# Moving a decay table's construction into an earlier stage, and reordering a layer change

## The chip, the core and the metric

The kernel runs on one core of a Trainium2 chip. The core has five engines with a queue each, and each takes its instructions in order: TensorE (PE, matrix products and transposes; PEld is its weight load), VectorE (DVE), ScalarE (ACT), GpSimd (POOL), and SyncE (SP), which mostly issues DMA transfers. ACT and POOL can issue DMAs as well. An instruction that waits for a semaphore holds back everything behind it on its engine. The metric is the device time of one execution in microseconds.

## The reference, cut to what matters

The input is x with 4 sequences of 2048 rows of 512 numbers. Four sublayers follow, each added to x.

```python
x = x + attn_a(layernorm(x), ...)   # causal linear attention, 16 heads of 64
x = x + ffn(layernorm(x), rhs)      # rows quantized to int8 levels, product with quantized rhs
x = x + attn_b(layernorm(x), ...)   # 16 heads, state of 16 x 32 with decay
x = x + ffn(layernorm(x), rhs)
```

Layer b's attention is a recurrence over time:

```python
decay = sigmoid(base_decay_logits)            # one number for each of 16 heads x 16 rows
M = M * decay + outer(g_t * k_t * scale, v_t)
y = einsum('bhr,bhrd->bhd', q_t, M)
```

In chunks of 128 steps it needs powers of the decay: a chunk's queries and keys are multiplied by powers of it, or of its inverse.

## The kernel before, in words

The program runs two layers one after the other: `layer_a_mild` (attention a and the first ffn), then `layer_b_mild` (attention b and the second ffn). A tile scheduler places the instructions on the engines: it keeps each engine's work near the order in which it is written, but moves instructions by its own estimate of when they can start. Line numbers in this text (L126, L804) are those of the kernel before.

Layer a works on 16 blocks of 512 rows (`TA`), each as 4 row tiles of 128 (`NTA`). For each block it loops over 8 pairs of heads, `hp`. A pair has a short list of steps from `attend` (keys, scores, update, weigh, outputs); `spread` puts other work between them, the list `fill`: the next pair's features (`pk`, `pq`), the values (`pv`), the projection of the block before (`po`). In the middle of a block the next block's rows enter (`enter_row`: statistics, normalization) and are turned. The statistics end on POOL: `rs`, by an add (L126) and a power (L127). DVE then normalizes with it (L131). DVE also evicts the features: `kT` and `qT` (L804), which PE's scores `pss` (L888) read. POOL adds up the states `within` (L914). In block 0, the ffn's weights are loaded and quantized as well (`load_part`, `quantize_part`).

The ffn on a row tile is `ffn_levels` on DVE (normalize, largest magnitude, levels `f_q`), then a turn of `f_q` by a DMA on SP's queue (L676), the product `pf` (L681), `f_y` on DVE (L683) and the residual add on POOL (L684). For the last block these four come one after the other behind the last projections: the drain. There the weights' denominators come by way of DRAM (`rec`, then two broadcast loads), and the block is stored to `mmid` (L998) at the end.

Layer b works on 32 blocks of 256 rows (`TB`), 2 row tiles (`NTB`) and 2 groups of 8 heads (`G`) each. Its tiles lie on the memory of layer a's, so a load can wait for layer a's last use of that memory. Before its loop comes a prologue: loads of rows (`xb`), of query and key weights (`m_qT`, `m_kT`), gates, low-rank weights, small constants, values and output weights; then normalization and transposes of blocks 0 and 1, `fill_tables`, and block 0's features (`pr`, L1222), gates (`pg`), low-rank products (`pl`, L1255) and values (`pvb`).

`fill_tables` builds five tables for each group: `up` and `down` (powers 0 to 128, ascending and descending), `inv` (powers of the inverse to 64), `tq` and `tk` (put together from those). It doubles: each step multiplies the columns known so far by the last of them, a per-partition scalar:

```python
nc.vector.tensor_scalar(
    tab[:, g, n + 1 : 2 * n + 1], tab[:, g, 1 : n + 1],
    tab[:, g, n : n + 1], None, ALU.mult,
)
```

Of the kernel before, what the change touches and what calls it, by code (L numbers as in the profile page):

```python
# [33 lines left out]
G = 2  # L34
# [7 lines left out]
QB = 128  # L42
NQ = P // QB


@with_exitstack
def hybrid_block_kernel(ctx: ExitStack, tc: tile.TileContext, t: dict, out: bass.AP):
# [584 lines left out]

    class Block:
# [39 lines left out]
    def ffn_product(pool, bank, x, q, s1):  # L673

        qT = pool.tile([P, KC, P], BF16, name="f_qT", bufs=2)
        nc.sync.dma_start_transpose(qT, q)  # L676

        def product():
            pf = bank([P, D], F32, name="pf", tag="mm")
            for c in range(KC):  # L680
                nc.tensor.matmul(pf, qT[:, c, :], rq[:, c, :], start=(c == 0), stop=(c == KC - 1))  # L681
            y = pool.tile([P, D], F32, name="f_y", bufs=1)
            nc.vector.scalar_tensor_tensor(y, pf, s1, rscale, ALU.mult, ALU.mult)  # L683
            nc.gpsimd.tensor_tensor(x, x, y, ALU.add)  # L684

        return [product]
# [28 lines left out]
    def join_halves(dst, turned):  # L715

        nc.scalar.copy(  # L717
            dst.bitcast(U16).rearrange("p n (t two) -> p n t two", two=2),
            turned.rearrange("p (two n) t -> p n t two", two=2),
        )  # L720

    def layer_a_mild():
        with ExitStack() as es:
# [268 lines left out]
            def levels(B, i):  # L992
                row = B.x[:, i, :]
                B.mul[i] = ffn_product(pool, bank, row, *ffn_levels(pool, row))

            def store(B):
                m = dram.tile([TA, D], F32, name=f"mmid_{B.n}")
                nc.sync.dma_start(rows(m, 0, TA), B.x)  # L998
# [13 lines left out]
            for n in range(len(at)):  # L1012
# [6 lines left out]
                for hp in range(NP):  # L1019
# [18 lines left out]
                    if more and 0 <= hp - 2 < NTA:  # L1038
                        enter_row(after, hp - 2)
                    for place, f in zip((6, 7, 13, 15), weights):  # L1040
# [12 lines left out]
                if n:  # L1053
                    store(prev)
                prev = B
                B = after if more else None

# [3 lines left out]
            levels(prev, 0)  # L1061
            run(row[1][4:])
            levels(prev, 1)
            run(row[2][4:] + row[3][:4] + prev.mul[0])
            levels(prev, 2)
            run(row[3][4:] + prev.mul[1])
            levels(prev, 3)
            run(prev.mul[2] + prev.mul[3])
            store(prev)

    def layer_b_mild():
        with ExitStack() as es:

            late = es.enter_context(tc.tile_pool(name="mb_l", bufs=1, reuse_waits="tile"))
            soon = es.enter_context(tc.tile_pool(name="mb_s", bufs=1, reuse_waits="tile"))
            rowp = es.enter_context(tc.tile_pool(name="mb_r", bufs=2, reuse_waits="tile"))
            w = es.enter_context(tc.tile_pool(name="mb_w", bufs=1, reuse_waits="tile"))
# [5 lines left out]
            def load_x(n):  # L1083
                b, blk = at[n]
                x = rowp.tile([P, NTB, D], F32, name="xb", bufs=6)

                queue = nc.scalar if n < 2 else nc.sync
                queue.dma_start(x, rows(mids[b, blk * TB // TA], blk * TB % TA, TB))
# [8 lines left out]

            first_rows = [row_tiles()]
            xs = [load_x(n) for n in range(2)]
            wp = {"q": load_weight(soon, "m_qT", D), "k": load_weight(soon, "m_kT", D)}  # L1100
            wg = load_weight(soon, "b_gT", G * P)
            low = {}
# [3 lines left out]
            small = {}  # L1106
            for name in ("b_gb", "b_decay", "head4", "diag", "causal"):
                small[name] = w.tile(list(t[name].shape), F32, name=f"m_{name}")
                nc.sync.dma_start(small[name], t[name])
            nc.sync.dma_start(wv, t["b_vT"].rearrange("(c p) n -> p c n", p=P))  # L1110
            out_b, ln_g, ln_b = (load_row(w, name) for name in ("b_out_b", "b_ln_g", "b_ln_b"))
            nc.sync.dma_start(wo, t["b_oT"].rearrange("(c p) n -> p c n", p=P))
            H2 = QB // 2
            up = w.tile([P, G, P + 1], F32, name="up")
            down = w.tile([P, G, P + 1], F32, name="down")
            inv = w.tile([P, G, H2 + 1], F32, name="inv")
            lam = w.tile([P, G], F32, name="lam")
            ilam = w.tile([P, G], F32, name="ilam")
            tq = w.tile([P, G, QB], F32, name="tq")
            tk = w.tile([P, G, NQ, P], F32, name="tk")  # L1120

            def fill_tables():

                nc.scalar.activation(lam, small["b_decay"], AF.Sigmoid)
                nc.vector.reciprocal(ilam, lam)
                nc.vector.memset(up[:, :, 0:1], 1.0)
                nc.vector.memset(inv[:, :, 0:1], 1.0)
                nc.vector.memset(down[:, :, P : P + 1], 1.0)
                nc.vector.tensor_copy(up[:, :, 1:2], lam.unsqueeze(2))
                nc.vector.tensor_copy(inv[:, :, 1:2], ilam.unsqueeze(2))  # L1130
                nc.vector.tensor_copy(down[:, :, P - 1 : P], lam.unsqueeze(2))
                n = 1
                while n < P:
                    for g in range(G):
                        for tab, last in ((up, P), (inv, H2)):
                            if n < last:
                                nc.vector.tensor_scalar(
                                    tab[:, g, n + 1 : 2 * n + 1], tab[:, g, 1 : n + 1],
                                    tab[:, g, n : n + 1], None, ALU.mult,
                                )  # L1140
                        nc.vector.tensor_scalar(
                            down[:, g, P - 2 * n : P - n], down[:, g, P - n : P],
                            down[:, g, P - n : P - n + 1], None, ALU.mult,
                        )
                    n *= 2


                nc.gpsimd.memset(tk, 0.0)
                nc.vector.tensor_copy(tq[:, :, H2:QB], up[:, :, 0:H2])
                nc.vector.tensor_copy(tq[:, :, H2 - 1 : H2], ilam.unsqueeze(2))  # L1150
                n = 1
                while n < H2:
                    for g in range(G):
                        nc.vector.tensor_scalar(
                            tq[:, g, H2 - 2 * n : H2 - n], tq[:, g, H2 - n : H2],
                            tq[:, g, H2 - n : H2 - n + 1], None, ALU.mult,
                        )
                    n *= 2
                for j in range(NQ):
                    m = QB * j + H2  # L1160
                    nc.vector.tensor_copy(tk[:, :, j, 0:m], down[:, :, P - m : P])
                    nc.vector.tensor_copy(tk[:, :, j, m : m + H2], inv[:, :, 0:H2])

# [11 lines left out]
            def enter_row(B, i):  # L1175

                if i == 0:
                    blk = at[B.n][1]
                    B.cs = []
                    for name in ("cos", "sin2"):  # L1180
                        c1 = rowp.tile([P, TB], F32, name=f"m_{name}", bufs=3)
                        queue = nc.scalar if B.n < 2 else nc.sync
                        queue.dma_start(c1, t[name][:, blk * TB : (blk + 1) * TB])
                        B.cs.append(c1.unsqueeze(1).to_broadcast([P, 2, TB]))
# [6 lines left out]
            def turn_row(B, i):  # L1191
                dst = B.xnT[:, :, i * P : (i + 1) * P]
                if B.n > 1:
                    join_halves(dst, B.halves[i])
                else:
                    transpose_rows(bank, dst, B.xr[:, i, :])
                nc.gpsimd.tensor_tensor(B.x[:, i, :], B.x[:, i, :], ln_b, ALU.add)
# [70 lines left out]
            def prepare(B, g):  # L1268
# [4 lines left out]
                A.k1 = pool.tile([P, NTB, NQ, P], F32, name=f"k1{g}", bufs=1)  # L1273
                nc.vector.tensor_tensor(
                    A.k1,
                    k.rearrange("p (i s) -> p i s", s=P).unsqueeze(2).to_broadcast([P, NTB, NQ, P]),
                    tk[:, g, :, :].unsqueeze(1).to_broadcast([P, NTB, NQ, P]), ALU.mult,
                )
                qs = pool.tile([P, NTB * NQ, QB], F32, name="qs", bufs=1)
                nc.vector.tensor_tensor(  # L1280
                    qs, q.rearrange("p (j s) -> p j s", s=QB),
                    tq[:, g, :].unsqueeze(1).to_broadcast([P, NTB * NQ, QB]), ALU.mult,
                )
                A.q1 = pool.tile([P, NTB * NQ, 4, QB], F32, name=f"q1{g}", bufs=1)
# [12 lines left out]
            def chunk(B, i, g):  # L1297
# [10 lines left out]
                def scores():  # L1308

                    A = B.prep[g]  # L1310
                    ps = [bank([P, NQ, 4, QB], F32, name="ps", tag="s") for _ in range(2)]
                    for j in range(NQ):
                        for half in range(2):
                            r = slice(half * 64, (half + 1) * 64)
                            nc.tensor.matmul(  # L1315
                                ps[half][:, j, :, :], A.k1[r, i, j, :], A.q1[r, NQ * i + j, :, :],
                                start=True, stop=True,
                            )
                    C.a = pool.tile([P, 2, 4, P], F32, name="ab")
                    for half in range(2):  # L1320
                        nc.vector.tensor_tensor(
                            C.a[:, half, :, :].rearrange("p h (j s) -> p h j s", s=QB),
                            ps[half].rearrange("p j h s -> p h j s"),
# [245 lines left out]
```

## Time and profile before

| | us |
|---|---|
| median of 3 runs | 4071.2 (4069.48 to 4073.05) |
| the profiled execution's own time | 4069.52 |
| its span, first to last instruction | 4067.7 |
| PE busy in the span | 3971.8 |
| DVE / ACT / POOL busy | 2334.7 / 876.2 / 1486.8 |
| layer a's last block stored (`mmid`, issued) | 2446.8 |
| layer b's block 1 begins on PE | 2504.3 |

Times in the text are microseconds from the start of the span. A row of the timeline gives start, duration, engine, line, operation, the tile written and the tiles read; in brackets how long the engine was idle before it and what ended that. The chain of waits is followed back from the last instruction: at each step to what released it. The granted clock is that of TensorE, 1.00 at full speed; it was 0.991 on the mean of the run.

### The profile page before, as it was taken

The page shows a single profiled execution, that of the slowest core. Times are in us where ns is not written, and L with a number is a line of the kernel's source. Part 1 is how long each engine was busy: PE and PEld are TensorE (multiplying, and loading weights), DVE is VectorE, ACT ScalarE, POOL GpSimd, SP SyncE. Part 2 cuts the span into 40 slices and gives each one's busy share as a digit, 9 for nine tenths or more (in the row PEclk, how much of TensorE's full clock was granted, in tenths as well). Part 3 has the DMA queues.
Part 4 walks back from the last instruction along what each step waited for, and adds up shares of the span by engine and source line. Part 5 has one row for each costly group of instructions (what it writes and reads, how often), then busy time and mean ns, then how long its engine had stood idle before and what let it go on. Part 6 is the DMA issues. An engine that isn't in the chain of part 4 may idle for free.

```text
span 4067.7 us, 53656 instructions
## 1 busy us (share of the span) xinstructions
PE 3971.8 (98%) x20821; PEld 2147.3 (53%) x20821; DVE 2334.7 (57%) x4556; ACT 876.2 (22%) x1420; POOL 1486.8 (37%) x2527
## 2 busy tenths in 40 slices
PE   8999999999999999999999987999999999999997
PEld 4554554555555555555555544555555555555553
DVE  4455555555555555555555454666666666666665
ACT  2122222221221222222122111222222222222221
POOL 3223323323333323323332223444444454444443
PEclk9999999999999999999999998999999999999998
DMA  4112212212212222221221123112211121221211
GB/s 135 32 39 58 64 36 62 60 38 64 55 43 64 54 54 52 54 66 38 54 66 39 39 65 108 47 47 49 51 47 47 47 50 48 50 50 47 53 32 29
DMA packets 432041, 217.25 MB, mean 53 GB/s; under 512 B 363808, under 2 KB 376992, under 8 KB 431776
## 3 DMA queue, kind: packets, MB, share of 16 engines
q1 hardware_dynamic: 430656, 212.16, 21.3%
q8 instruction: 165, 2.70, 0.3%
q10 hardware_dynamic: 1120, 1.57, 0.1%
q14 instruction: 100, 0.82, 0.1%
HBM read 91.49 MB, written 34.08 MB: 31 GB/s over the span
## 4 chain that ended last, share of the span: by engine, by line
PE 82%; DVE 8%; POOL 7%; issue 1%; DMA 1%; ACT 0%; SPq 0%; POOLq 0%; ACTq 0%; DVEq 0%
PE pk L648 11%; PE pv L648 11%; PE pq L648 11%; PE po L648 10%; PE pr L1222 8%; PE py L648 5%; PE pss L888 3%; PE pn L974 3%; PE pvb L648 3%; PE pn L968 3%; PE pf L681 2%; PE pu L904 2%; PE ps L1315 2%; PE pl L1255 2%; PE pg L648 2%; POOL rs L127 2%
## 5 line engine op out<-in xcount | busy, mean ns | idle before, releaser
L648 PE MATMUL pq<-xnTa,a_Wq 128*128 128x512 f32 x1024 | 492.2, 608 | 0.0
L648 PE MATMUL pk<-xnTa,a_Wk 128*128 128x512 f32 x1024 | 491.0, 604 | 0.0
L648 PE MATMUL pv<-a_Wv,xnTa 128*128 128x512 f32 x1024 | 475.3, 602 | 2.9 <-ACT xnTa L141 2.9
L648 PE MATMUL po<-a_Wo_sb,oT 128*128 128x512 f32 x1024 | 467.1, 601 | 6.1 <-DVE oT L950 6.1
L126 POOL TENSOR_SCALAR rs<-mv 128x1 f32<-128x1 f32 x320 | 70.7, 221 | 764.2 <-DVE mv L125 763.9
L914 POOL TENSOR_TENSOR within<-state,u 64x64 f32<-64x64 f32 x256 | 154.5, 603 | 524.6 <-ACT u L909 515.0
L648 PEld LDWEIGHTS po<-a_Wo_sb,oT 128*128 128x128 f32 x1024 | 189.5, 191 | 234.3 <-issue 220.9
L648 PEld LDWEIGHTS pv<-a_Wv,xnTa 128*128 128x128 f32 x1024 | 188.4, 190 | 233.7 <-issue 223.7
L648 PEld LDWEIGHTS pq<-xnTa,a_Wq 128*128 128x128 f32 x1024 | 181.4, 189 | 193.1 <-issue 182.8
L648 PEld LDWEIGHTS pk<-xnTa,a_Wk 128*128 128x128 f32 x1024 | 184.6, 190 | 180.8 <-issue 158.8
L909 ACT COPY u<-pu 128x256 f32<-128x256 f32 x128 | 47.6, 372 | 1027.6 <-PE pu L904 1016.7
L1222 PE MATMUL pr<-xnTb,m_kT_sb 128*128 128x256 f32 x1024 | 259.5, 392 | 0.0
L1222 PE MATMUL pr<-xnTb,m_qT_sb 128*128 128x256 f32 x1024 | 252.8, 390 | 0.0
L648 PE MATMUL pvb<-b_vT_sb,xnTb 128*128 128x512 f32 x512 | 242.3, 606 | 0.0
L894 DVE TENSOR_TENSOR sm<-pss,causal 128x512 f32<-128x512 f32 x256 | 164.3, 683 | 119.9 <-PE pss L888 119.9
L648 PE MATMUL py<-b_oT_sb,yT 128*128 128x512 f32 x512 | 231.6, 594 | 0.0
L717 ACT COPY kr<-turned 128x1024 uint16<-128x1024 uint16 x120 | 139.3, 1161 | 425.4 <-DMA turned<-planes 425.4
L1222 PEld LDWEIGHTS pr<-xnTb,m_qT_sb 128*128 128x128 f32 x1024 | 187.5, 190 | 77.0 <-issue 44.5
L1222 PEld LDWEIGHTS pr<-xnTb,m_kT_sb 128*128 128x128 f32 x1024 | 184.4, 189 | 51.2 <-issue 20.0
L1361 POOL TENSOR_TENSOR state_b<-pairs,m_diag 128x256 f32<-128x256 f32 x128 | 98.3, 768 | 293.5 <-DVE pairs L1339 187.1
L127 POOL TENSOR_TENSOR rs<-rs,neg_half 128x1 f32<-128x1 f32 x320 | 193.7, 606 | 23.8
L838 DVE TENSOR_TENSOR xa<-po,xa 128x512 f32<-128x512 f32 x64 | 44.1, 689 | 260.1 <-PE po L648 260.1
(158 smaller groups left out, 6412.5 us busy)
## 6 DMA issues: line engine op xcount, KB each, us to landing
wide<-rec SPq DMA_DIRECT2D x124, 256.0 KB, 3.7
mmid<-xa SPq DMA_DIRECT2D x16, 1024.0 KB, 4.3
out<-xb SPq DMA_DIRECT2D x32, 512.0 KB, 2.8
xa<-in_x SPq DMA_DIRECT2D x15, 1024.0 KB, 6.3
xb<-mmid SPq DMA_DIRECT2D x30, 512.0 KB, 3.8
turned<-planes SPq DMA_TRANSPOSE x304, 3.1
m_cos<-in_cos SPq DMA_DIRECT2D x30, 128.0 KB, 2.3
m_sin<-in_sin SPq DMA_DIRECT2D x30, 128.0 KB, 2.3
```

Source lines behind the costliest of these rows:

```text
L127: nc.gpsimd.tensor_tensor(rs, rs, neg_half[:, :n], ALU.pow)
L648: nc.tensor.matmul(held[0], lhs(), rhs(), start=(n == 0), stop=(n == len(pairs) - 1))
L681: nc.tensor.matmul(pf, qT[:, c, :], rq[:, c, :], start=(c == 0), stop=(c == KC - 1))
L717: nc.scalar.copy(dst.bitcast(U16).rearrange("p n (t two) -> p n t two", two=2), turned.rearrange("p (two n) t -> p n t two", two=2),)
L888: nc.tensor.matmul(ps[h][:, i, :], k[r, chunks[i]], q[r, chunks[i]], start=True, stop=True)
L894: nc.vector.tensor_tensor(s, ps[h], causal.unsqueeze(1).to_broadcast([P, NTA, P]), ALU.mult)
L904: nc.tensor.matmul(pu[r, i, :], A.kr[:, i, r], v()[:, i, vh[h]], start=True, stop=True, skip_group_check=True,)
L914: nc.gpsimd.tensor_tensor(A.before[i + 1][r, r], A.before[i][r, r], u[r, i, :], ALU.add)
L968: nc.tensor.matmul(pn[:, i, :], A.before[i], q[:, chunks[i]], start=(i == 0), stop=False, skip_group_check=True,)
L974: nc.tensor.matmul(pn[r, i, :], v()[:, i, vh[h]], A.sm[h][:, i, :], start=False, stop=True, skip_group_check=True,)
L1222: nc.tensor.matmul(pr[:, half, :], wp[name][:, c, lo : lo + P], B.xnT[:, c, :], start=(c == 0), stop=(c == KC - 1),)
L1361: nc.gpsimd.tensor_tensor(st.rearrange("p (q c) -> p q c", c=2 * DB), pairs[:, g, :].unsqueeze(1).to_broadcast([P, HG // 2, 2 * DB]), smal ...
```

## The change

It has four parts.

1. `fill_tables` goes. A class `Powers` builds `up`, `down`, `inv` and `tq` in layer a's block 0, on POOL, in a piece of the tile `wide`; the steps are put between those of pairs 0 to 2 (`braid` mixes them into `fill`). SP stores the result to DRAM, and layer b loads it in one transfer. Layer b makes `tk` alone, by two copies on DVE.
2. In the drain, `f_q` is turned by PE and an ACT copy (`by_dma` false), not by a DMA; the steps are regrouped; the last store of `mmid` is issued by POOL.
3. Layer b's loads are reordered, and all stand on SP: rows, query weight and angles of block 0 first, tables and values later, the output weight last. `xb` and the angles get a pool of their own.
4. The prologue works block 0 first; block 1's rows enter between block 0's groups, and the residual adds (`residuals`) come after. The constants `QB`, `NQ` (128 and 1) go, which changes no shape.

The diff, cut to its core:

```diff
-    def ffn_product(pool, bank, x, q, s1):
+    def ffn_product(pool, bank, x, q, s1, by_dma=True):
         qT = pool.tile([P, KC, P], BF16, name="f_qT", bufs=2)
-        nc.sync.dma_start_transpose(qT, q)
+        if by_dma:
+            nc.sync.dma_start_transpose(qT, q)
         def product():
+            if not by_dma:
+                transpose_rows(bank, qT, q, BF16)
...
+    class Powers:
+        sizes = (P + 1, P + 1, H2 + 1, P)
+        size = G * sum(sizes)
...
+        def fill(self, tab, lam, ilam):
+            up, down, inv, tq = self.views(tab)
+            self.home = dram.tile([P, self.size], F32, name="powers_d")
+            copy, times = nc.gpsimd.tensor_copy, nc.gpsimd.tensor_scalar
...
+            while n < P:
+                for g in range(G):
+                    todo = [(up[:, g, n + 1 : 2 * n + 1], up[:, g, 1 : n + 1], up[:, g, n : n + 1]),
+                            (down[:, g, P - 2 * n : P - n], down[:, g, P - n : P], down[:, g, P - n : P - n + 1])]
+                    if n < H2:
+                        todo += [(inv[:, g, n + 1 : 2 * n + 1], inv[:, g, 1 : n + 1], inv[:, g, n : n + 1]),
+                                 (tq[:, g, H2 - 2 * n : H2 - n], tq[:, g, H2 - n : H2], tq[:, g, H2 - n : H2 - n + 1])]
+                    for dst, src, by in todo:
+                        steps.append(lambda dst=dst, src=src, by=by: times(dst, src, by, None, ALU.mult))
+                n *= 2
+            def store():
+                copy(tq[:, :, H2:P], up[:, :, 0:H2])
+                nc.sync.dma_start(self.home, tab[:, : self.size])
...
+                    if n == 0 and hp == 0:
+                        tab = pool.tile([P, 2, TA], F32, name="wide", bufs=1).rearrange("p j t -> p (j t)")
+                        lam, ilam = (tab[:, powers.size + j * G : powers.size + (j + 1) * G] for j in range(2))
+                        nc.sync.dma_start(lam, t["b_decay"])
+                        nc.scalar.activation(lam, lam, AF.Sigmoid)
+                        nc.vector.reciprocal(ilam, lam)
+                        table = powers.fill(tab, lam, ilam)
+                    if n == 0 and hp < 3:
+                        fill = braid(fill, table[len(table) * hp // 3 : len(table) * (hp + 1) // 3])
...
-            levels(prev, 0)
+            levels(prev, 0, False)
...
-            run(row[2][4:] + row[3][:4] + prev.mul[0])
-            levels(prev, 2)
-            run(row[3][4:] + prev.mul[1])
-            levels(prev, 3)
+            run(row[2][4:] + prev.mul[0])
+            levels(prev, 2, False)
+            run(row[3] + prev.mul[1])
+            levels(prev, 3, False)
             run(prev.mul[2] + prev.mul[3])
-            store(prev)
+            store(prev, nc.gpsimd)
...
-                queue = nc.scalar if n < 2 else nc.sync
-                queue.dma_start(x, rows(mids[b, blk * TB // TA], blk * TB % TA, TB))
+                nc.sync.dma_start(x, rows(mids[b, blk * TB // TA], blk * TB % TA, TB))
...
+            xs = [load_x(0)]
+            wp["q"] = load_weight(soon, "m_qT", D)
+            css = [angles(0)]
+            xs.append(load_x(1))
+            wp["k"] = load_weight(soon, "m_kT", D)
             wg = load_weight(soon, "b_gT", G * P)
...
+            tab = w.tile([P, powers.size], F32, name="powers")
+            nc.sync.dma_start(tab, powers.home)
+            up, down, inv, tq = powers.views(tab)
+            tk = w.tile([P, G, P], F32, name="tk")
             nc.sync.dma_start(wv, t["b_vT"].rearrange("(c p) n -> p c n", p=P))
...
-            fill_tables()
-            first = get(0)
-            for g in range(G):
-                run(features(first, "q", g) + features(first, "k", g) + gates(first, g) + keys(first, g))
-                run(values(first, g))
-                prepare(first, g)
+            nc.vector.tensor_copy(tk[:, :, 0:H2], down[:, :, H2:P])
+            nc.vector.tensor_copy(tk[:, :, H2:P], inv[:, :, 0:H2])
+            for g in range(G):
+                run(features(first, "q", g))
+                enter_row(second, g)
+                run(features(first, "k", g) + gates(first, g))
+                turn_row(second, g)
+                run(values(first, g) + keys(first, g))
+                prepare(first, g)
+            for B in (first, second):
+                for i in range(NTB):
+                    residuals(B, i)
```

The memset of `state_b`, which opens layer b's block loop, is not edited.

## The prediction

> **What bounds the kernel now.** I read the page's busy times first, then the busy time by stretches around the two places that the diff touches, then the chain and the timeline there.
>
> ```profile
> PE 3971.8 (98%) x20821; PEld 2147.3 (53%) x20821; DVE 2334.7 (57%) x4556; ACT 876.2 (22%) x1420; POOL 1486.8 (37%) x2527
> ```
>
> TensorE (PE) is the bound; it idles 4067.7 - 3971.8 = 96 us in all. So the edit can gain only where PE idles, and a cost counts only where PE comes to wait. Busy time by stretches (us, busy us and count per engine, granted clock, DMA share, GB/s), where layer a ends:
>
> ```profile
> 2405.00:2410.00 5.00, 0.88 (x3) 0.05 (x1) 0.00 (x0) 0.00 (x0) 0.00 (x0) 0.85 0.89 191
> ...
> 2435.00:2440.00 5.00, 1.03 (x4) 0.27 (x4) 3.12 (x7) 0.00 (x0) 2.55 (x4) 0.58 0.91 332
> 2440.00:2445.00 5.00, 1.89 (x4) 0.43 (x4) 0.29 (x1) 0.00 (x0) 0.00 (x0) 0.50 0.80 253
> 2445.00:2450.00 5.00, 0.00 (x0) 0.00 (x0) 0.59 (x5) 0.00 (x0) 2.12 (x4) 0.50 0.90 314
> 2450.00:2455.00 5.00, 1.12 (x4) 0.72 (x4) 3.68 (x9) 0.00 (x0) 1.71 (x4) 0.50 1.05 400
> 2455.00:2460.00 5.00, 0.00 (x0) 0.00 (x0) 0.10 (x2) 0.42 (x1) 0.00 (x0) 0.50 0.92 313
> ```
>
> From 2400 to 2500 PE is busy 61 of 100 us, partly at half clock: some 39 us idle, against 57 in the other 3968. The chain of waits in that stretch (start, us, what):
>
> ```profile
> 2439.84 2.83 DMA f_qT<-f_q
> 2442.72 1.90 PE pf L681 x4
> 2444.71 0.75 DVE f_y L683
> 2445.54 1.26 POOL xa L684
> 2447.26 11.49 DMA b_oT_sb<-in_b_oT
> 2459.14 3.98 DMA b_out_b_row<-in_b_out_b
> ```
>
> The reader sees a turn by DMA, then loads: SP's queue holds layer b's loads behind layer a's last turns and store, and GpSimd's (POOL's) first residual add waits for a bias row. Then DVE fills the tables, 2466.88 to 2481.3, while PE waits ("issue" before `pl` at 2482.65). Block 1 of layer b starts on PE at 2504.31. The other place is layer a's first block (timeline; the bracket is idle time before, and who ended it):
>
> ```profile
> 42.77 0.22 POOL L126 TENSOR_SCALAR rs<-mv 128x1 f32<-128x1 f32 x1 [9.79 <-DVE mv L125]
> 43.67 0.55 DVE L131 TENSOR_SCALAR xn<-xa,mv,rs 128x512 f32<-128x512 f32 x1 [0.36 <-POOL rs L127]
> 44.13 0.68 DVE L804 TENSOR_SCALAR qT<-pq 128x512 f32<-128x512 f32 x1
> 44.87 1.16 PE L888 MATMUL pss<-qT,kT 64*128 64x128 f32 x16
> ```
>
> POOL makes `rs`, DVE normalizes with it, evicts `qT` next, and PE's scores `pss` follow within 0.1 us: no slack from `rs` to PE.
>
> **The change, part by part.** All by the time axis of the profiled run, 4069.5 us with a span of 4067.7.
>
> Tables in block 0. Added on POOL: 3 memsets, 4 small copies, 52 scalings of 1 to 64 columns, one 128x128 copy; one sigmoid on ACT, one reciprocal on DVE, a 1 KB load and a 462 KB store on SP. The memsets (0.1 us each) lie in POOL's 1.1 us wait before 8.66: nothing. The load stands behind `xa` on SP and moves the next two loads by an issue slot, 1 to 2 us; startup's transfers end at 39 and the first of these tiles is read at 41.9: nothing. The sigmoid stands between ACT's copy ending at 36.5 and `kr` at 43.20: nothing, unless the decays came after 43; they arrive at about 37 (that queue lands in order; 36.5 to 39.2). The reciprocal is one 0.17 us step near 41.9. But in the built order (how the changed program's instructions stand on each engine) 51 of the 52 scalings stand on POOL ahead of that `rs`, and the last before its power step. POOL's cover is only 37 to 42.77.
>
> Price p of one scaling: two independent `rs<-mv` back to back take 0.38 us, 0.16 apart; dependent ones start 0.30 apart; the mean is 221 ns. The table's steps depend on the fourth before, and each has its scalar in memory, which no row shows. I take 0.23, bounds 0.16 and 0.31. Columns: about 0.9 us for all (the 128x128 select took 0.29). DVE's scan (1.23 us at 40.06) blocks POOL for 1.2: two `within` took 1.97 us instead of 0.70 beside a copy and a scan at 51.64. So `rs` ends at 37 + 1.2 + 59p + 0.9 + 0.65 = 39.75 + 59p, and `pss` starts 1.23 later (44.87 - 43.64). Stall = 59p - 3.9: 5.5 at 0.16 (5.9, since the reciprocal then holds), 9.7 at 0.23, 14.4 at 0.31. Behind the waiting `xn` on DVE stand `qT`, `planes`, `qc`, `sm`; behind `pss` all of PE. I take +9.7.
>
> A rule that speaks against this move: the Trainium skill, "GPSIMD Engine Reference", § 4.1 Engine selection, sends elementwise work to VectorE, POOL being about 2x slower on two-input work. DVE ran these steps 0.135 us apart (2475.4 to 2478.9). Twice that, 0.27, gives a stall of 12.0 instead of 9.7 and a net of -4.0 for the -6.3 below. The same section counts one-input work as nearly line rate, so I keep the row.
>
> Clock. An idle of 4.95 us before `pl` at 2482.65 left half clock (1.12 us for 0.65). "TensorE: Matmul & The Clock Gate", § Why this matters, warns against gaps over some 3 us; so the stall brings about 4 us at half clock, 1.9 us lost. The row beside it: PE waited 1.25 + 0.29 + 0.29 us for `within` soon after (53.66 to 55.22), a time set by POOL and DVE, so I count the loss as hidden there. Without that cover the net is -4.4.
>
> The drain. Four turns leave SP (2.8 us each in the chain); PE gets four groups of transposes (0.39), ACT four copies (0.58). Row 3's projection now ends behind row 0's transposes, copy and product at 2433.05 (before 2431.65). Then `xa`, `st`, `mv`, `rs`, `xn` to 2436.35; `f_y` of row 2 waits on POOL's add of row 1 till 2438.5; levels to 2440.65; transposes, copy, product to 2443.5, `f_y` ends about 2444.5 (before 2445.46), POOL's add about 2445.85. Gain there 1 us.
>
> Loads. With the turns gone, SP issues the loads from about 2404.5 instead of 2433.8. What block 0 needs (x, query, key and gate weights, low-rank weights, tables: 5.5 MB) lands by about 2421 at the 370 GB/s of startup; the weight for values waits for the last projection, 2433, and lands by 2439. They stand behind the broadcasts of `rec` in the same queue; if they slowed these, layer a's last projection would start 0 to 1 us later.
>
> The new wait. The last `mmid` store is now issued by POOL, and the built order puts behind it the memset of `state_b`, which waits for the store's landing (its memory is layer a's), and then all `rs` of layer b. No POOL-issued DMA is in the trace. Nearest row: stores of this size from SP land in 4.3 us. I take 5.1 (bounds 4.3 and 8): landing at 2451.0. Memsets 0.53 + 0.12, `rs` 0.87, `xr` 0.55: first transposes at 2453.2, against 2452.87 before. So nothing is gained up to there. After it: second `rs`, `xr`, transposes 1.1 (half clock), copy 0.6: query features at 2457.0. 16 passes, the first 4 us at half clock, to 2462.4; then keys 3.45, gates 1.8, transposes 0.55, values 3.5, `pl` 1.9, the second half 3.45 + 3.45 + 1.8 + 0.55 + 3.5 + 1.9: block 1 at 2488.3 against 2504.3. Gain 16.0; bounds 13 to 18.
>
> Taken off DVE there: the whole fill, 14.4 us, now two copies of 0.21 beside PE's features. ACT's table load (1.28 us at 2459.58) moves to the first gate at 2467.7, whose bank PE needs back at 2473.6: nothing, and 1 us if gates came 5 us later. The residual adds on POOL move behind the features, beside PE. SP's remaining loads wait for the store too, and land by some 2461; the first reader, block 2's statistics, stands behind `xs_k` at 2467: hidden; if 6 us later they would delay the first `k`. In the steady blocks the instructions are the same.
>
> Sum: +9.7 - 16.0 = -6.3. The median of the runs, 4071.2, lies 1.7 above the profiled run: forecast 4064.9, about 4065.
>
> **The rivals.**
> Cheap tables: p near 0.16 and the store landed in 4.3 us: +5.9 - 17 = -11, 4060. For it: independent steps. Against it: a scalar operand each.
> Late store: software issue makes it 8 us or more: gain 13, net -3 or less, 4068. For it: no such DMA in the trace.
> Slower: POOL's queue ahead of `rs`. From p = 0.34 the stall eats the gain; from 0.475 the kernel is over 8 us slower; at 0.60 (the mean of the first `within`, beside DVE) the stall is 31.5 and the time 4087. Against it: the same `within` takes 0.35 undisturbed.
> The change does not do what it says: no, the built order has no table step left on DVE in layer b.
>
> **How the numbers follow.** 0.2% is 8.1 us, about what a measurement here can tell. The likeliest case (0.52; -2 to -10) gives 4065; cheap tables 0.24, late store 0.13, slower 0.11. Faster by over 8.1: cheap tables and the lower part of the likeliest, 0.38. Slower by over 8.1: most of the last, 0.09. Same: 0.53. Range 4057 to 4075: the low end leaves out the best of the cheap case, the high end holds p up to 0.40.
>
> **What would show it.** Right: POOL solid from 37 to about 52 in block 0, `rs` at about 53, PE idle about 10 us before `pss`, then half clock; at layer b no table steps, `state_b`'s memset waiting for `mmid`, query features about 11 us after POOL's last add of layer a, PE without a gap from there, block 1 some 42.5 us after that add. Wrong: PE idle under 5 or over 15 us at 45; features waiting for a load; PE idle in the first features for DVE.

## The result, and the profile after

The changed kernel takes 4074.5 us (median of 12 runs, 4073.2 to 4078.2), the kernel before 4071.3 (12 runs, 4069.5 to 4073.1): a ratio of 1.001, 95% interval 1.0002 to 1.0018. It is slower by about 3 us where -6 was forecast. The profiled execution of the changed kernel is its slowest run, 4078.2 us with a span of 4076.4, and that of before stands 1.8 us below its median; so the two traces differ by 8.7 us where the medians differ by 3.2.

First the page's line of busy times. PE's idle time is 4076.4 - 3980.7 = 95.7 us, as much as before (96): what was won in one place was given back elsewhere. Busy time grew by 8.9 us; it counts PE's products at half clock and its new turns too.

```profile
PE 3980.7 (98%) x20837; PEld 2150.1 (53%) x20837; DVE 2327.2 (57%) x4496; ACT 879.1 (22%) x1424; POOL 1512.7 (37%) x2587
```

Next, layer a's first block in the timeline (start, us, engine, what; the bracket is idle time before and who ended it). To be read against the shown rows of before, in which `rs` began at 42.77 and `pss` at 44.87; this execution started 1.25 us later.

```profile
37.90 0.32 POOL L760 COPY wide<-wide 128x2 f32<-128x2 f32 x2 [4.64 <-ACT wide L1104]
38.20 6.53 POOL L770 TENSOR_SCALAR wide<-wide 128x1 f32<-128x1 f32 x20
...
41.31 1.23 DVE L928 TENSOR_TENSOR_SCAN qc<-go,kT 128x512 f32<-128x512 f32 x1
...
44.94 6.33 POOL L770 TENSOR_SCALAR wide<-wide 128x32 f32<-128x32 f32 x20
...
51.45 3.42 POOL L770 TENSOR_SCALAR wide<-wide 128x8 f32<-128x8 f32 x11
54.80 0.26 POOL L125 TENSOR_SCALAR rs<-mv 128x1 f32<-128x1 f32 x1
...
55.96 0.55 DVE L130 TENSOR_SCALAR xn<-xa,mv,rs 128x512 f32<-128x512 f32 x1 [11.33 <-POOL rs L126]
56.42 0.68 DVE L863 TENSOR_SCALAR qT<-pq 128x512 f32<-128x512 f32 x1
...
57.16 2.08 PE L947 MATMUL pss<-qT,kT 64*128 64x128 f32 x16 [11.02 <-DVE qT L863]
```

The chain is the one that the prediction followed: 51 table steps on POOL, then `rs`, `xn`, `qT`, and PE idle for 11.02 us. The 51 steps take 6.53 + 6.33 + 3.42 = 16.28 us, 0.319 each. A row of the timeline merges steps of several widths and shows the first one's shape. By width, all 52 steps look like this (after the bar busy us and mean ns of one):

```profile
L770 POOL TENSOR_SCALAR wide<-wide 128x1 f32<-128x1 f32 x8 | 2.2, 299 | 0.0
L770 POOL TENSOR_SCALAR wide<-wide 128x8 f32<-128x8 f32 x8 | 3.3, 443 | 0.0
L770 POOL TENSOR_SCALAR wide<-wide 128x32 f32<-128x32 f32 x8 | 2.8, 388 | 0.0
L770 POOL TENSOR_SCALAR wide<-wide 128x64 f32<-128x64 f32 x4 | 1.8, 481 | 0.0
```

The mean of the eight columns holds one step of 1.24 us, at 41.42 beside DVE's scan. The other steps begin 0.25 us apart with 1 column, 0.33 with 32 and 0.42 to 0.44 with 64, and 0.297 on the mean.

After the stall `pss` takes 2.08 us instead of 1.16: the granted clock is 0.50 from 57.0 to 59.2, and 1.00 again from 62.9.

Then the layer change, in the chain of waits (start, us, what):

```profile
2462.70 0.76 DVE f_y L692
2463.46 0.07 issue
2463.52 1.27 POOL xa L693
2464.79 0.29 issue
2465.08 0.02 POOLq L1455
2465.10 0.00 issue
2465.10 5.00 DMA mmid<-xa
2470.10 0.06 issue
2470.15 0.52 POOL state_b L1455
2470.67 0.14 POOL pairs L1456
2470.82 0.21 POOL rs L125
...
2475.95 8.78 PE pr L1259 x32
```

The new wait is where it was expected: POOL's store lands 5.0 us after its issue, the zeroing of `state_b` waits for it, and layer b's first `rs` stands behind the zeroing. Query features start 11.2 us after POOL's last add, and no table step is left on DVE.

Last, an instruction that the prediction took to be unchanged: POOL's product `ke` in layer b's steady blocks (groups by form, as above), first of the kernel before, then of the changed one.

```profile
L1290 POOL TENSOR_TENSOR ke<-k,down 128x256 f32<-128x256 f32 x61 | 44.2, 725 | 13.1 <-DVE k L1263 11.4 <-DVE f_sc L665 1.7
```

```profile
L1327 POOL TENSOR_TENSOR ke<-k,powers 128x256 f32<-128x256 f32 x61 | 49.8, 817 | 13.1 <-DVE k L1300 11.4 <-DVE f_sc L670 1.7
```

The same instruction on the same shapes takes 92 ns more. By the issue times of `out` on SP, layer b's blocks follow each other every 49.08 us instead of 48.88; two issues in a row, first before, then changed:

```profile
2735.49 0.40 SPq L1390 DMA_DIRECT2D out<-xb  x1
2784.38 0.40 SPq L1390 DMA_DIRECT2D out<-xb  x1
```

```profile
2738.75 0.39 SPq L1420 DMA_DIRECT2D out<-xb  x1
2787.83 0.40 SPq L1420 DMA_DIRECT2D out<-xb  x1
```

To see where the 8.7 us lie, the program is cut at points that every kernel has: the first `pk` on PE in block 0 (about 36), SP's issue of the first `rec` store (about 105), that of the last one (about 2401), the start of layer b's block 1 on PE, the end. All from the timeline; us.

| kernel | first `pk` | to first `rec` | to last `rec` | to block 1 of b | to the end |
|---|---|---|---|---|---|
| before | 35.7 | 69.3 | 2296.3 | 103.0 | 1563.4 |
| changed | 37.0 | 81.5 | 2299.0 | 89.2 | 1569.7 |
| tables on 32 bytes | 36.3 | 81.8 | 2298.8 | 87.2 | 1563.6 |
| table in the drain | 38.1 | 70.3 | 2297.4 | 87.1 | 1567.5 |
| late zeroing | 36.9 | 81.3 | 2297.5 | 83.8 | 1569.8 |
| before, `down` moved 8 bytes | 37.2 | 69.3 | 2297.1 | 103.3 | 1569.1 |
| all three edits | 36.5 | 70.3 | 2296.3 | 81.7 | 1563.0 |
| turned by DMA | 36.2 | 81.2 | 2301.1 | 96.0 | 1568.4 |
| filled by DVE in layer b | 36.1 | 69.4 | 2297.4 | 87.8 | 1564.0 |
| scaling by a constant | 37.0 | 77.6 | 2296.5 | 87.9 | 1568.6 |
| filled by DVE, late zeroing | 36.3 | 69.3 | 2298.0 | 85.5 | 1562.6 |

The first and the third stretch wander by 2 to 5 us between kernels that are alike there (by 1.5 and 0.8 between the kernel before and its moved twin), so nothing is read from them. The other three are plain: +12.2 in block 0, -13.7 to -15.8 at the layer change where it is as the change left it, and +4 to +6 over layer b's blocks in every kernel with the slow `ke`.

### The profile page after: what moved, and what is told of

Read it like the earlier page. It is cut to its first block, busy times and chain, and to the rows that moved or that the text cites. A ratio compares the mean times of both kernels' runs of the same rounds, so it can differ in the third digit from the quotient of the medians.

```text
span 4076.4 us, 53690 instructions
## 1 busy us (share of the span) xinstructions
PE 3980.7 (98%) x20837; PEld 2150.1 (53%) x20837; DVE 2327.2 (57%) x4496; ACT 879.1 (22%) x1424; POOL 1512.7 (37%) x2587
## 3 DMA queue, kind: packets, MB, share of 16 engines
q0 software_dynamic: 272, 1.05, 0.1%
## 4 chain that ended last, share of the span: by engine, by line
PE 80%; DVE 7%; POOL 6%; DMA 3%; ACT 1%; issue 1%; SPq 0%; POOLq 0%; ACTq 0%; DVEq 0%
PE pv L653 11%; PE pk L653 11%; PE pq L653 11%; PE po L653 10%; PE pr L1259 8%; PE py L653 5%; PE pss L947 3%; PE pn L1033 3%; PE pvb L653 3%; PE pn L1027 3%; PE pf L690 2%; PE pu L963 2%; PE ps L1351 2%; PE pg L653 2%; DVE st L123 2%; PE pl L1292 2%
```

## The experiments

Each ratio is to the kernel before, run beside the experiment (its medians there: 4071.7 to 4072.1); differences in microseconds are to the changed kernel's 4074.5 unless the text says otherwise.

**The start of `down`.** The table `down` had a tile of its own before. Packed behind `up` in one tile, its two groups are read from 12 and 16 bytes past a multiple of 32; before, from 4 and 8. The edit puts each table on a multiple of 32 bytes:

```
-        size = G * sum(sizes)
+        starts = (0, 264, 528, 664)
+        size = 664 + G * P
```

> The changed kernel with its four tables each started on a multiple of 32 bytes (three small memsets fill the gaps); nothing else differs. Theory: in the changed kernel the POOL product ke takes 0.91 and 0.73 us for the two groups of a block of layer b where it took 0.82 and 0.64 before, because the table `down` now starts 12 and 16 bytes past a multiple of 32 instead of 4 and 8, and what follows it (planes of ke, then ab, then PE) costs 0.19 us in each of some 30 blocks. Then ke is back at 0.82 and 0.64, a block of layer b takes 48.88 instead of 49.08 us, and the time falls by 5.7 us, to about 4069. Rival: the 0.19 us come from k and ke themselves, which stand 32 bytes elsewhere, or are chance of that execution: ke stays at 0.91 and 0.73, or the block stays at 49.08, and the time stays at 4074.5.

Measured: 4070.0 us (13 runs, 4067.4 to 4073.1, where the changed kernel's 12 lie from 4073.2 to 4078.2); ratio to before 0.9997, interval 0.9988 to 1.0005. So 4.5 us of the changed kernel's time are gone; layer b's blocks are at 48.88 us, and the stretch to the end at 1563.6. The group of `ke` in this kernel:

```profile
L1329 POOL TENSOR_TENSOR ke<-k,powers 128x256 f32<-128x256 f32 x61 | 44.3, 726 | 13.1 <-DVE k L1302 11.4 <-DVE f_sc L670 1.7
```

The converse, on the kernel before, where nothing else of the change is present:

```
-            down = w.tile([P, G, P + 1], F32, name="down")
+            down = w.tile([P, 2 + G * (P + 1)], F32, name="down")[:, 2:].rearrange("p (g n) -> p g n", g=G)
```

> The kernel before, with only the table `down` moved by 8 bytes within a slightly longer tile, so that its two groups are read from 12 and 16 bytes past a multiple of 32, as in the changed kernel. Theory: ke goes from 0.82 and 0.64 to 0.91 and 0.73 us, layer b's block from 48.88 to 49.07, the time from 4071.3 to 4077. Rival: no change, 4071.3: then the place of `down` is not the cause.

Measured: 4077.2 us (13 runs), ratio 1.0013, interval 1.0005 to 1.0021. Eight bytes make the kernel before 5.5 us slower than its own runs beside it. The groups of `ke`, and who PE waited for between 2600 and 3900 (us in total, times, longest), in this kernel; the wait of the kernel before in the second fence:

```profile
L1290 POOL TENSOR_TENSOR ke<-k,down 128x256 f32<-128x256 f32 x61 | 49.8, 817 | 13.1 <-DVE k L1263 11.4 <-DVE f_sc L665 1.7
...
PE pyT L1354 <- DVE ab L1321: 11.4, 54, 0.3
```

```profile
PE pyT L1354 <- DVE ab L1321: 7.3, 44, 0.2
```

POOL's later `ke` makes DVE's `planes<-ke` later by 0.09 us, `ab` stands some steps behind it on DVE, and PE's `pyT` waits for `ab`. That cover was already used up before the change (7.3 us of waits there), so a tenth of a microsecond twice a block came through; the growth of these waits, 4.1 us, is most of the 5 us that the blocks lose in the stretch. The `k` and `ke` tiles stood elsewhere in the changed kernel as well; in this run every tile but `down` keeps its address, and it gives the whole effect.

Two single runs with other starts, again on the kernel before with only `down` moved:

> The kernel before with `down` moved by 16 bytes: its two groups are read from 20 and 24 bytes past a multiple of 32. Known so far: 4 and 8 are quick (0.82 and 0.64 us for ke), 12 and 16 slow (0.91 and 0.73). If the cost is one more row of 32 bytes touched beyond some place in it, 20 and 24 are slow too: 0.91 and 0.73, a block of 49.07 us. If 12 and 16 alone are bad (the middle of a row), ke is at 0.82 and 0.64 and the block at 48.88.

> The kernel before with `down` moved by 24 bytes: the first group is read from 28 bytes past a multiple of 32, the second from a multiple of 32 itself. If the place in the row of 32 bytes decides, the first is slow (0.91) and the second quick (0.64 or less), and a block takes about 48.98 us; if only 12 and 16 are bad, both are quick and the block takes 48.88.

The times are 4074.3 and 4079.9 us, and the blocks follow each other every 48.90 and 49.07 us. Their groups, 16 bytes first, 24 bytes second:

```profile
L1290 POOL TENSOR_TENSOR ke<-k,down 128x256 f32<-128x256 f32 x61 | 44.3, 726 | 13.2 <-DVE k L1263 11.4 <-DVE f_sc L665 1.7
```

```profile
L1290 POOL TENSOR_TENSOR ke<-k,down 128x256 f32<-128x256 f32 x61 | 49.8, 816 | 13.2 <-DVE k L1263 11.4 <-DVE f_sc L665 1.7
```

Starts at 20 and 24 are quick, 28 and 0 slow, for both groups (0.91 and 0.73 in the slow case, 0.82 and 0.64 in the quick one). Of the two guesses on record, neither holds in full: 20 and 24 being quick speaks against "beyond some place in the row", a slow start at 0 against "only 12 and 16". Taken together the starts with remainder 4 or 8 to 16 bytes were quick and those with 12 or 0 slow. Why is not shown; one instruction with one shape was measured.

**The place of the table steps.** The same steps on the same engine, tied to POOL's last state update so that the scheduler can't hoist them:

```
-                    if n == 0 and hp < 3:
-                        fill = braid(fill, table[len(table) * hp // 3 : len(table) * (hp + 1) // 3])
...
+            nc.gpsimd.tensor_scalar(z, state[:, NP - 1, 0 : 2 * G], 0.0, None, ALU.mult)
+            nc.gpsimd.tensor_tensor(z, z, both, ALU.add)
+            run(powers.fill(tab, z[:, 0:G], z[:, G : 2 * G]))
```

> The changed kernel with the same 59 table steps on POOL, but in layer a's drain, behind POOL's last state update at about 2415 (a multiply by zero of that state ties them to it); the tables' store is issued by POOL too. The decays are still loaded and turned by sigmoid and reciprocal in block 0. Theory: the 12.2 us lost by the end of block 0's first pairs were the stall behind the table; POOL sits idle for 22 us in the drain, the table takes 19 us there and costs nothing: 4074.5 - 12 = 4062, with 1.3 us of late start remaining if the small load delays the startup. Rival: the table does not fit, since the idle is 22.5 us and the store's issue and the first rs stand behind it: then the first row's rs is 2 to 5 us late and the gain is 7 to 10 us. Other rival: block 0's loss is not the table's order on POOL but the longer startup: gain under 3.

Measured: 4062.2 us (10 runs), ratio 0.9975, interval 0.9966 to 0.9985; 12.3 below the changed kernel. In its timeline the 52 steps stand in POOL's idle stretch (17.63 us with three that DVE's work held up), and the first `rs` of the drain comes right behind them:

```profile
2404.43 17.63 POOL L770 TENSOR_SCALAR va<-va 128x1 f32<-128x1 f32 x52
...
2422.60 0.78 POOL L775 DMA_DIRECT2D powers_d<-va  x1 [0.31 <-POOL va L774]
2423.41 0.27 POOL L125 TENSOR_SCALAR rs<-mv 128x1 f32<-128x1 f32 x1
```

Block 0 is back at 70.3 us, and the layer change at 87.1. So the order on POOL was the loss of block 0, all but 1.0 us; that much stays there when the decays' load, sigmoid and reciprocal remain in block 0 (70.3 in two kernels that have them, 69.3 to 69.4 in those that don't). What holds it was not traced.

**The price of a step.** Every scaling by a constant in place of a column of the table:

```
-   times(dst, src, by, None, ALU.mult)
+   times(dst, src, 0.75, None, ALU.mult)
```

> The changed kernel with every one of the 52 scalings by a constant (0.75) in place of a column of the table; the tables then hold other numbers, the rest of the work is the same. It measures what makes a scaling cost 0.31 to 0.33 us on POOL where the sum took 0.23. Theory: the scalar that each reads from memory, since 52 scalings run at 0.32 whether they have 1 or 64 columns: without it they run at 0.16 to 0.22 us, the table ends 5 to 8 us earlier, and PE's stall before pss falls from 11.0 to 3 to 6 us. Rival: 0.3 us is what POOL takes for one of these steps in any case (each is issued, run and written back before the next): the table still takes 17 us and the stall stays at 11.

The tables then hold other numbers; the work is the same. One run: 4069.4 us. The timeline of block 0, and two of its widths:

```profile
38.38 4.92 POOL L770 TENSOR_SCALAR wide<-wide 128x1 f32<-128x1 f32 x20
...
53.27 2.08 PE L947 MATMUL pss<-qT,kT 64*128 64x128 f32 x16 [7.06 <-DVE qT L863]
```

```profile
L770 POOL TENSOR_SCALAR wide<-wide 128x1 f32<-128x1 f32 x8 | 1.5, 216 | 0.1
L770 POOL TENSOR_SCALAR wide<-wide 128x64 f32<-128x64 f32 x4 | 1.5, 392 | 0.0
```

The 51 steps take 4.92 + 4.60 + 2.46 = 11.98 us, 0.235 each, and the stall falls to 7.06. Here too one step stands 1.28 us beside DVE's scan; the others begin 0.17 us apart with 1 column and 0.34 to 0.36 with 64. The truth lies between the two theories: the scalar read from memory costs 0.08 to 0.09 us at every width, and the rest is what a step costs in any case. That 1 and 64 columns take the same, as the expectation says, was a misreading of the merged rows: 64 columns cost some 0.17 us more than 1, with or without the scalar.

**The wait for the store.** Layer b's zeroing behind the first two `rs` on POOL:

```
+            done = first.xr[:, NTB - 1, :]
+            nc.gpsimd.tensor_scalar(state.rearrange("p g n -> p (g n)"), done, 0.0, None, ALU.mult)
...
-                if B and B.first:
+                if n and B and B.first:
```

> The changed kernel, but layer b's first zeroing of state_b and pairs is a multiply by zero of the second normalized row, so that it stands on POOL behind the first two rs instead of ahead of them; the store is still issued by POOL. Theory: the first two rs waited only for the landing of the store (5.0 us of DMA, 0.6 of memsets): the first transposes start 1.8 us after POOL's last add instead of 7.6, and the time falls by 5.5 to 6, to about 4069. Rival: another thing is late by then, a load (x, cosines, the tables for tk) or DVE's row statistics: the gain is under 3 us, and the features wait for it.

Measured: 4070.9 us (13 runs, 4066.3 to 4072.1), ratio 0.9994, interval 0.9986 to 1.0003. Its timeline:

```profile
2462.65 1.00 POOL L1057 DMA_DIRECT2D mmid<-xa  x1 [0.31 <-POOL xa L693]
2463.68 0.25 POOL L125 TENSOR_SCALAR rs<-mv 128x1 f32<-128x1 f32 x1
...
2465.32 1.09 PE L139 MATMUL pt<-ident,xr 128*128 128x128 f32 x4 [5.19 <-DVE mv L124]
```

The transposes start 3.0 us after POOL's last add (2462.33) instead of 7.6: issuing the store holds POOL for 1.0 us, which the expectation had left out. Block 1 starts 37.2 us after that add where it was 41.9, a gain of 4.7; the time fell by 3.6 us. In this profile some 2 us were lost again in front of it, in the wait for the broadcast of `rec` (see the point on the layer change below).

**The turns.** The drain's levels turned by DMA again:

```
-            levels(prev, 0, False)
+            levels(prev, 0)
```

(and likewise rows 1 to 3.)

> The changed kernel with the drain's levels turned by DMA again, as before; all else as changed. Theory: the change gained some 13.6 us at the layer change, most of it since SP no longer holds the loads behind the turns: with the turns back, three stand ahead of the loads in SP's queue and the first waits for row 0's levels, so the weights land late again, the features wait for the query weights or x, and the time rises by 6 to 10 us, to 4081 to 4084. Rival: the gain is the table fill gone from DVE and the order of the loads; then the turns cost only the difference of their own chain, 1 to 2 us each at the last row: 4076.

Measured: 4083.1 us (7 runs), ratio 1.0028, interval 1.0017 to 1.0039: 8.6 above the changed kernel, as much as the theory had it, but by another last wait. From the timeline (SP's queue) and the chain:

```profile
2440.48 11.74 SPq L683 DMA_TRANSPOSE f_qT<-f_q  x3
2452.59 0.38 SPq L1157 DMA_DIRECT2D xb<-mmid  x1
```

```profile
2466.66 10.36 DMA mmid<-xa
2477.01 0.06 issue
2477.07 0.52 POOL state_b L1455
```

The three turns hold SP until 2452.6, so layer b's loads run between 2453 and 2477. The features don't wait for a weight: POOL's store shares the DMA engines with these loads (busy shares of 0.92 to 1.05, 269 to 364 GB/s, in the four stretches of 5 us from 2455 to 2475) and takes 10.4 us instead of 5.0. Between the two profiles the layer change differs by 96.0 - 89.2 = 6.8 us, and 5.4 of them are this store. So turning by PE pays mostly through the loads that it lets go early; that they are what slows the store is read from the shares, and no run tests it alone.

**The change without its table move.** Tables filled by DVE in layer b's prologue, each on 32 bytes, nothing on POOL or by way of DRAM:

```
-            copy, times = nc.gpsimd.tensor_copy, nc.gpsimd.tensor_scalar
+            copy, times = nc.vector.tensor_copy, nc.vector.tensor_scalar
...
-            nc.sync.dma_start(tab, powers.home)
+            nc.scalar.activation(lam, small["b_decay"], AF.Sigmoid)
+            nc.vector.reciprocal(ilam, lam)
+            run(powers.fill(tab, lam, ilam))
```

> The changed kernel without its table move: the tables are built in layer b's prologue by DVE, straight in place and on multiples of 32 bytes, in the gap in which PE works on the first query features; no table step on POOL, nothing by way of DRAM. Theory: block 0 gets its 12.2 us back and layer b's blocks their 0.19, as in the two single edits, and DVE's 52 steps (0.135 us each before, 7 us) lie beside 9 us of features: 4074.5 - 12.3 - 4.5 + 0 to 3 = 4058 to 4061, so that moving the tables to block 0 was a loss by itself and the rest of the change a gain of 10 to 13. Rival: the fill holds up xc and xs, and pl behind them, as it did before (4.95 us of idle before pl): 4063 to 4066.

Measured: 4057.1 us (5 runs), a little under what was expected; ratio 0.9965, interval 0.9951 to 0.9978. The fill stands here on DVE:

```profile
2456.64 10.86 DVE L771 TENSOR_SCALAR powers<-powers 128x1 f32<-128x1 f32 x52
```

It lies beside PE's query and key features (2458.66 to 2468.3), and the layer change is no longer for it than with the tables from DRAM (87.8 against 87.1 and 87.2). With PE's turns and the new order of loads DVE's fill had become free where it stood; moving it to block 0 could only cost.

The old fill was also longer than its steps. In the kernel before, six of them took 1.31 us each instead of 0.21, each ending with one of POOL's residual adds:

```profile
2467.49 0.21 DVE L1141 TENSOR_SCALAR down<-down 128x1 f32<-128x1 f32 x1
...
2469.25 1.31 DVE L1141 TENSOR_SCALAR down<-down 128x2 f32<-128x2 f32 x1
2469.27 1.27 POOL L1198 TENSOR_TENSOR xr<-xr,b_out_b_row 128x512 f32<-128x512 f32 x1
```

Six times 1.1 us is nearly half of the 14.4 us that the prediction takes off DVE (an estimate; no run moves the adds alone). Most of DVE's other steps begin 0.12 to 0.16 us apart.

**The versions that come out of it.** All three edits together, and the fill by DVE with the late zeroing:

> The three single edits together: tables on multiples of 32 bytes, the table steps in the drain, the zeroing behind the first two rs. If the three costs are independent the gains add up, 4.5 + 12.3 + 3.6 = 20.4 us off 4074.5: 4054. Rival: in the drain POOL's table (22 us of its idle) and the store issued behind it delay something that the earlier start then waits for (the tables' load, wanted for tk): 4057 to 4060.

> The changed kernel with the tables filled by DVE in layer b's prologue, in place and on multiples of 32 bytes, and with layer b's zeroing behind the first two rs: the changed order of loads and PE's turns without any table work on POOL or by way of DRAM. If the gains add: 4057.1 - 3.6 to 5 = 4052 to 4053.5, as good as the version with all three edits and simpler. Rival: with the features some 6 us earlier, DVE's 7 us of table steps no longer fit beside them and hold up xc, xs and pl: 4054 to 4056.

Measured: all three 4052.0 us (5 runs), ratio to before 0.995, interval 0.9937 to 0.9964; the other 4053.6 (5 runs), 0.9957, interval 0.9943 to 0.997. Both beat the kernel before by 18 to 20 us. The three costs were independent to within 2 us: the sum of the single gains asked for 4054. In the second, DVE's 52 steps take 11.6 us, and PE waits 0.92 us for `xr` at 2468. Its layer change is 2.3 us shorter than with the fill by DVE alone, where the late zeroing saves 5.4 beside the tables in the drain (87.1 and 81.7). So a part of the rival is true.

## Why the prediction was wrong, point by point

**Block 0: right in kind, 2.5 us short.** The mechanism, the order on POOL, the readers behind `rs` and the stall were as forecast; 9.7 was the term, 11.0 of idle and 12.2 in all what it measured. From the first copy to the end of `rs` POOL took 18.0 us (37.90 to 55.93), where the formula has 1.2 + 59 x 0.23 + 0.9 + 0.65 = 16.3; it began 0.35 us earlier than forecast.

The price of a narrow step was nearly right, 0.25 against 0.23, though by some luck: the row that it was taken from has a constant as its second operand. A step with a constant and 1 column begins 0.167 us after the one ahead, like the 0.16 of that row, and the scalar in memory adds the rest. What was too small is the columns: 0.9 us was put down for all of them, and the 52 steps take 2.3 us more than 52 of one column. Against that, the 59 counts three memsets that the prediction itself had placed at 8.66, and it prices the small copies like scalings though they take 0.12 to 0.17 us each. The scan on DVE held POOL up as forecast, by 0.9 us instead of 1.2.

The rule that was weighed there, the Trainium skill, "GPSIMD Engine Reference", § 4.1 Engine selection, gave 0.27 as twice DVE's 0.135. With the held-up steps left out, DVE's fill in layer b has a step every 0.136 us on the mean and POOL's in block 0 every 0.297, a ratio of 2.2. So this step, with one tensor and one scalar column as inputs, lay near what the section says of two inputs, and not near line rate.

**The clock after the stall: half hidden.** The forecast hid 1.9 us of half clock behind the `within` waits. From the start of `pss` to the end of the products `pk` behind it PE took 5.7 us instead of 3.1, a loss of 2.6. The waits, in the stretch 30 to 110, first before, then changed:

```profile
PE pn L968 <- POOL within L914: 1.8, 3, 1.3
```

```profile
PE pn L1027 <- POOL within L973: 0.6, 2, 0.3
```

So 1.2 were absorbed, and 12.2 - 11.0 = 1.2 came through, 2.4 of the 2.6. The Trainium skill, "TensorE: Matmul & The Clock Gate", § Why this matters for your kernels, warns of idle gaps over some 3 us, and after this one of 11.0 us the loss came.

**The layer change: right.** -16.0 forecast; -13.7 in the profile of the changed kernel, -15.1 to -15.8 in four other kernels whose layer change is as long as the change left it (87.1 to 87.9 us: tables on 32 bytes, table in the drain, scaling by a constant, filled by DVE). The store was put at 5.1 us and took 5.0; features at 11.2 us after POOL's last add and they came at 11.2; block 1 at 42.5 after it, and 41.9. The one miss is in front of it: the broadcast of `rec` came late in some executions. From the store of `rec` to DVE's first product with it pass 9.3 us before, 10.7 in the profile of the changed kernel, 11.3 with the late zeroing, 9.0 to 9.7 in the others. The loads that SP now issues right behind the broadcasts are the likely reason, since both late ones have them; but six of the others have them too, so it is not shown. The 0 to 1 us of the forecast should have been 0 to 2.

**Layer b's blocks: the step that failed.** "In the steady blocks the instructions are the same" was priced at nothing. They are the same, and one of them is not as quick: +0.19 us in each of some 30 blocks, 5.7 us, which no rival of the prediction named. The cause is the packing of the tables into one tile, which moved the start of `down` by 8 bytes. With the other terms as they stood on record (+9.7 and -16.0) this alone would have made a forecast of -0.6; with block 0's 12.2 and a layer change of -15.5 the sum is +2.4, against the measured +3.2. So the steady blocks took the gain away, and what block 0 cost beyond its forecast made the loss. The measured 4074.5 lies inside the stated range, but by luck: its upper end was drawn for table steps of up to 0.40 us.

## What to carry to other kernels

When a change moves or repacks tiles, list the instructions of the steady blocks that read them and compare their mean times with the kernel before, even where the code is the same; a tenth of a microsecond counts wherever the trace already shows short waits in each block. Before work is put on an engine because it looks idle, read what stands behind it in that engine's order and who reads that; and price a step by a row with the same kind of operands and the same width. A move is worth judging against the rest of its own change: here the new load order had already made the old place of the work free.

## What the runs showed of the hardware

POOL's `TENSOR_SCALAR` on 128 partitions, from one start to the next, takes 0.25 us with a scalar from memory and 1 column, 0.33 with 32 columns and 0.42 to 0.44 with 64; with a constant 0.17, 0.25 and 0.34 to 0.36. POOL and DVE held each other up: a POOL step beside DVE's scan of 1.23 us took 1.24, and DVE steps beside POOL's adds of 1.27 took 1.31 instead of 0.21. POOL's product of 128x256 with a table repeated over two chunks takes 0.09 us longer when the table's rows start 12 or 0 bytes past a multiple of 16 than with 4 or 8. A store of 1 MB issued by POOL holds POOL for 0.9 to 1.0 us. It lands after 4.7 to 5.0 us where layer b's loads had gone ahead of it, and after 10.4 where they ran beside it.
